# Loading routed tokens as 32-channel squares and turning them on VectorE instead of TensorE

## The chip, the cores and the metric

The kernel runs on one core of one Trainium2 chip. The metric is device time in microseconds (us) of one execution. Engines are named as the profile names them: PE is TensorE, DVE VectorE, ACT ScalarE, POOL GpSimd, SP the SyncE queue that issues most DMAs.

## What is computed

One graph layer and one transformer block over N = 4096 nodes with C = 256 channels, in fp32:

```python
h = layernorm(x);  h = concat(lin1(h), adj @ lin2(h) / degree)
h = layernorm(h)
h = h + wo(causal_attention(rmsnorm(h)))      # 4 heads, 2 kv heads, width 64, rope
g = top2(softmax(router(rmsnorm(h))))         # 8 experts
out = h + sum_e g[e] * w2[e](silu(w1[e] x) * w3[e] x),  x = rmsnorm(h), hidden width 682
```

Every token goes through two of the eight experts. The change concerns how a token's 256 channels get from the residual stream to the first matmul of its expert, where the channels have to lie on the partitions.

## The kernel before

**Stages.** The graph part ends at about 510 us of the profiled execution, attention at about 1060, and the experts at about 1522. The order on each engine is written out by hand: every engine executes its instructions in the order in which the program emits them, and waits are placed where one needs another's result.

**Lists.** While attention finishes block by block, `inputs` writes the normalized rows (L174 is `normed`), `project` adds what the first half of the router gives (L907), `residual` adds the rows to the residual stream on POOL (L917), and POOL scatters each token by indirect DMA (L1060) into `lists` in DRAM, ordered by expert. One row of `lists` has ROW = 265 words: 256 channels, the token's number, and 8 gates.

**Groups.** The experts work on 42 groups in a fixed order `TURNS`: 25 of 256 tokens and 17 of 128. All tokens of a group belong to one expert, whose weights are read at an index that the core finds in a table (`make_table`). For turn k the SP queue issues `load13` (L1382, 1.4 MB), `load2` (L1388, 0.77 MB) and `load_rows` (L1399, one DMA: 128 tokens on the partitions, one or two tokens of 265 words each). Rooms for rows and weights rotate by five; in turn k the weights of k+5 and k+4 and the rows of k+4 are loaded. `begin_experts` issues the first ones.

**One turn.** The main loop calls, for turn k, `hidden(k)` or `hidden_seven(k)`, then `combine(k-1)`, then the loads, then `sums13`, which prepares a later group's weights on POOL.

- `prepare(k+1)` is called inside the hidden part of turn k. It turns the rows on PE, four transposes of 128x128 for 256 tokens and two for 128 (L1413, tile `tx` in PSUM), ACT scales both channel halves by the norm's weights into `xT` (L1419), and DVE picks the gate of the group's expert (`pick` L1427, `gt` L1432). At which point of turn k this happens depends on which PSUM bank is free (`early`, `free_bank`).
- `hidden(k)` multiplies `xT` with w1 and w3 (L1698), ACT applies silu (L1704), DVE multiplies (L1705; L1717 for the last 42 channels).
- `hidden_seven(k)` does the same for 13 of the 256-token groups (`SPLIT13`) with seven half-size products instead of eight (L1525). It needs sums of weights, made ahead by `sums13` on POOL (L1463 to L1466), and sums of tokens T1 to T4, made by `sums_x` within `prepare` on DVE (L1480), T1 from `xT` and the PSUM tile and the others from each other and the PSUM tile. Its products are copied and added by ACT (L1531) and DVE (L1563, L1564), and L1595 and its neighbours multiply with silu.
- `split` (L1612 to L1615), `sums2` (L1631 to L1634) and `seven_products` (PE L1655, DVE L1661 to L1667) do the second layer in the same manner for all groups of 256 in `SEVEN`.
- `combine(k)` scales by the gate into `y` (ACT L1765 or DVE L1771) and POOL adds the rows into `acc_dram` by a scattering indirect DMA (L1776), after a small memset (L1775) that paces it. A small DMA from `sent` (L1911) holds SP back until then.

The copy from `acc_dram` to `out` (L1923) is issued three turns before the end; the last groups scatter into `out` itself.

In most of the stage a 256-token group of `hidden_seven` is followed by one 128-token group, whose `prepare` readies the next 256 tokens; three times two 128-token groups follow one another.

Other names that are used below: L790 is attention's exponential on ACT, L792 its mask on POOL, L810 the running sums of the softmax on DVE, L824 the products with the values on PE, L311 the transposes of the rope tables on DVE (the only DVE transposes before), `acc<-a` L532 the product with adj.

Of the kernel before, what the change touches and what calls it, by code (L numbers as in the profile page):

```python
# [10 lines left out]
I32 = mybir.dt.int32  # L11
# [55 lines left out]
def fast_kernel(  # L67
# [618 lines left out]
    with (  # L686
# [14 lines left out]
        pt_all = sp.tile([P, 9 * 1024], F32, name="pt_all")  # L701
        late = sp.tile([P, 2 * (NF + 1) * GR + 4 * GR + 5 * 2 * ROW], F32, name="late")
        LATE_XT, LATE_ROWS = 2 * (NF + 1) * GR, 2 * (NF + 1) * GR + 4 * GR
        ring = [pt_all[:, n * 1024 : (n + 1) * 1024] for n in range(9)]
# [182 lines left out]


        def inputs(b):

            row = ax.tile([P, TB, ROW], F32, tag="row", name=f"row_{b}")
            for t in range(TB):
                normed(row[:, t, 0:C], b, t, rstd[b][:, t])
            flats[b] = row

        def project(b, tiles, rooms):
            if tiles[0] == 0:
                picks[b] = small("r_p", b)
            for t, ps in zip(tiles, rooms):
                for c in range(2):  # L900
                    nc.tensor.matmul(
                        ps[:, 0 : C + NE], ys[b, c][:, t * P : (t + 1) * P], wo_sb[:, c, :],
                        start=(c == 0), stop=(c == 1),
                    )
            for t, ps in zip(tiles, rooms):
                x2 = flats[b][:, t, 0:C]
                nc.vector.tensor_add(x2, x2, ps[:, 0:C])  # L907
                nc.vector.tensor_add(picks[b][:, t, :], ps[:, C : C + NE], first_lg[b][:, t, :])
# [7 lines left out]
        def residual(b):  # L916
            nc.gpsimd.tensor_add(res[b], res[b], flats[b][:, :, 0:C])  # L917
            put = nc.sync.dma_start(acc_blocks[b], res[b])
            lend(b, "res", 4)
            if b == ORDER[-1]:  # L920
                free(put, "first sums", "the tokens of the first groups are others")
                join(put, "last x")
# [449 lines left out]
        w2s = [a.rearrange("p (k c) -> p k c", k=NF + 1) for a in at2]  # L1372
        rows, hidden_of, inputs_of, expert_of, gates_of = {}, {}, {}, {}, {}

# [11 lines left out]
        def load2(k):  # L1386
# [4 lines left out]
            )  # L1391

        def load_rows(k):
            i = TURNS[k]
            n = halves(i)
            at = entry(table[0:1, 0, i : i + 1], NE * REG - (GR if i < NW else 0))
            r = late[:, LATE_ROWS + k % 5 * 2 * ROW : LATE_ROWS + (k % 5 + 1) * 2 * ROW]
            r = r.rearrange("p (h c) -> p h c", h=HALF)
            get = nc.sync.dma_start(  # L1399
                r[:, 0:n, :], lists[bass.ds(at, n * P), :].rearrange("(h p) c -> p h c", p=P)  # L1400
            )
            if i < NA:
                free(get, "late writes", "the rows of the first groups are whole by then")
                join(get, "first reads")
            rows[i] = r

        def prepare(k, pool=p_y, tag="y"):
            i = TURNS[k]
            n = halves(i)
            tr = pool.tile([P, 2, n, P], F32, tag=tag, name=f"tx_{i}")  # L1410
            for h in range(n):
                for c in range(2):
                    nc.tensor.transpose(  # L1413
                        tr[:, c, h, :], rows[i][:, h, c * P : (c + 1) * P], ident
                    )
            xT = late[:, LATE_XT + k % 2 * 2 * GR : LATE_XT + k % 2 * 2 * GR + 2 * n * P]
            xT = xT.rearrange("p (c i) -> p c i", c=2)
            for c in range(2):
                nc.scalar.activation(  # L1419
                    xT[:, c, :], tr[:, c].rearrange("p h i -> p (h i)"), AF.Copy,  # L1420
                    scale=ln2_sb[:, c : c + 1],
                )
            inputs_of[i] = xT
            if k in SPLIT13:
                sums_x(k, tr)
            pick = ex.tile([P, n, NE], F32, tag="pick", name=f"pick_{i}")
            nc.vector.tensor_mul(  # L1427
                pick, rows[i][:, 0:n, C + 1 : ROW],
                mine[:, i : i + 1, :].to_broadcast([P, n, NE]),
# [38 lines left out]

        def sums_x(k, tr):

            xT = inputs_of[TURNS[k]]
            room = kT[6 + SPLIT13.index(k) % 2].rearrange("p (n i) -> p n i", n=4)
            m = {f"T{n + 1}": room[:, n] for n in range(4)}
            for c in range(2):
                for h in range(2):
                    m[f"B{c + 1}{h + 1}"] = xT[:, c, h * P : (h + 1) * P]
            for dst, c, h, less in (
                ("T1", 0, 1, "B11"), ("T2", 1, 1, "T1"), ("T3", 1, 1, "B12"), ("T4", 1, 0, "T2"),
            ):
                nc.vector.scalar_tensor_tensor(  # L1480
                    m[dst], tr[:, c, h, :], ln2_sb[:, c : c + 1], m[less],
                    op0=ALU.mult, op1=ALU.subtract,
# [3 lines left out]
        def hidden_seven(k, step, behind):  # L1486
# [99 lines left out]
            if behind is not None:  # L1586
                prepare(behind, p_ms, "ms")
            gated(two)
# [83 lines left out]
        def hidden(k, step=None, behind=None):  # L1672
# [3 lines left out]
            hT = hTs[k % 2][:, :, 0:n]  # L1676
            free_bank = k >= SEVEN[0]
            early = n == P and not (k - 1 in SEVEN and k - 2 in SEVEN)

            for q in range(0, NF + 1, 2):  # L1680
# [27 lines left out]
                if q == 0 and behind is not None:  # L1708
                    if not free_bank:
                        prepare(behind)  # L1710
                    elif early:
                        prepare(behind, p_ms, "ms")
                if step and q < NF - 1:
# [5 lines left out]
            )  # L1719
            if behind is not None and free_bank and not early:  # L1720
                prepare(behind, p_ms, "ms")
            hidden_of[i] = hT
# [3 lines left out]
        def combine(k):  # L1726
# [34 lines left out]
            for h in range(n):  # L1761
# [8 lines left out]
                else:  # L1770
                    nc.vector.tensor_scalar(  # L1771
                        y[:, h, :], ps[h if last else 0][:, h, :], gt[:, h], None, op0=ALU.mult
                    )
                at = bass.IndirectOffsetOnAxis(ap=r[:, h, C : C + 1].bitcast(I32), axis=0)
                nc.gpsimd.memset(gap, 0.0)  # L1775
# [13 lines left out]
        def begin_experts():  # L1789
            make_table(NB - 1, True, 0, NA)  # L1790
            load_rows(0)
            load13(0)
            load_rows(1)
            load2(0)
            load13(1)
            load_rows(2)
            load2(1)
            load_rows(3)

# [38 lines left out]
        for b in ORDER[:-1]:  # L1840
# [9 lines left out]
        later.setdefault(PLACES - 2, []).append(  # L1850
            lambda: [prepare(0, p_ms, "ms")] + [nc.gpsimd.memset(t[:, NF, :], 0.0) for t in hTs]
        )
# [36 lines left out]
        for k in range(NM):  # L1889
# [24 lines left out]
            if k + 5 < NM:  # L1914
                load13(k + 5)
            if k + 4 < NM:
                load_rows(k + 4)
            if 0 < k < NM - 1:
# [13 lines left out]
def rare_groups(  # L1932
# [34 lines left out]
    for i in range(RARE):  # L1967
# [6 lines left out]
        w2_sb = sb.tile([P, NF + 1, C], F32, tag="w2", name=f"y_w2_{i}")  # L1974
        nc.sync.dma_start(w2_sb, w2[bass.ds(e, 1)].rearrange("o p k c -> p (o k) c"))
        tr = p_y.tile([P, 2, P], F32, tag="y", name=f"y_tr_{i}")
        xT = sb.tile([P, 2, P], F32, tag="xT", name=f"y_xT_{i}")
        for c in range(2):
            nc.tensor.transpose(tr[:, c, :], r[:, c * P : (c + 1) * P], ident)
            nc.scalar.activation(  # L1980
# [684 lines left out]
```

## Time and profile before

| | |
|---|---|
| median of 3 runs | 1532.09 us (1532.08 to 1533.21) |
| the profiled execution | 1532.31 us, of which 1530.5 span |
| PE busy | 1518.1 us, 99% |
| DVE, ACT, POOL busy | 1056.4, 555.6, 556.8 us |
| DMA moved | 212.16 MB in 69595 packets |
| loads of rows, L1399 | 42 on SP |
| transposes of tokens, L1413 | 134 on PE |

The page's rows for groups of instructions read: line, engine, operation, written tile, read tiles, shape, count, then busy microseconds and the mean nanoseconds of one, then the idle time of that engine just before them and what ended it. Rows of a single line give minimum, median and maximum in nanoseconds. Rows of a timeline read: start, duration, engine, line, operation, tiles, count, and in brackets the idle time before and its releaser. Rows of a stretch read: the stretch, its length, then the busy time of PE, PE's weight loads, DVE, ACT and POOL with instruction counts, the granted clock, the DMA engines' busy share, and GB/s.

### The profile page before, as it was taken

To read this page: it belongs to the slowest core of one execution; us is meant where nothing else is said; L and a number is where in the kernel's file an instruction comes from. 1 tells how busy PE (TensorE), PEld (TensorE's weight loads), DVE (VectorE), ACT (ScalarE), POOL (GpSimd) and SP (SyncE) were. 2 spreads that over 40 slices of the span, in tenths; PEclk is the share of its full clock that TensorE was granted. 3 is DMA by queue.
4 is the path that set the end of the run, shared out by engine and by line. 5 is a ranking of instruction groups with operands and counts; after the bars stand their busy time and mean duration, and the time that the engine had idled before them with its cause. 6 is when DMAs were issued, how large, how long until landed. Compare 5 with 4: busy or idle time off the path is not lost. (4 is left out here: it accounts for less than half of the span.)

```text
span 1530.5 us, 28132 instructions
## 1 busy us (share of the span) xinstructions
PE 1518.1 (99%) x10925; PEld 1122.9 (73%) x10925; DVE 1056.4 (69%) x2182; ACT 555.6 (36%) x989; POOL 556.8 (36%) x641
## 2 busy tenths in 40 slices
PE   9999999999999999999999999999999999999997
PEld 8888888888888544444444444358899999999996
DVE  7764665755755677779879878785565777677762
ACT  2102012021021455655665655653122433343341
POOL 2102022121221331374554553442424445545342
PEclk9999999999999999999999999999999999999999
DMA  6334444543544000010011011048777787787845
GB/s 240 131 130 151 160 141 148 161 153 127 179 141 151 5 1 23 22 58 30 30 58 37 28 38 36 23 166 297 220 204 219 225 275 254 225 274 248 271 129 134
DMA packets 69595, 212.16 MB, mean 139 GB/s; under 512 B 17898, under 2 KB 45930, under 8 KB 55818
## 3 DMA queue, kind: packets, MB, share of 16 engines
q1 hardware_dynamic: 55914, 191.99, 36.4%
q0 software_dynamic: 12720, 17.47, 6.5%
q8 instruction: 88, 1.44, 0.4%
q10 hardware_dynamic: 816, 0.79, 0.2%
q14 instruction: 57, 0.47, 0.1%
HBM read 184.48 MB, written 27.13 MB: 138 GB/s over the span
## 5 line engine op out<-in xcount | busy, mean ns | idle before, releaser
L782 PE MATMUL sc<-qT_all,kT 64*64 64x512 f32 (+3 forms) x2304 | 282.1, 557 | 0.5 <-ACT pt_all L790 0.3
L532 PE MATMUL acc<-a,g 128*128 128x256 f32 x1024 | 244.0, 379 | 0.0
L532 PEld LDWEIGHTS acc<-a,g 128*128 128x128 f32 x1024 | 193.5, 190 | 31.8 <-issue 6.7
L782 PEld LDWEIGHTS sc<-qT_all,kT 64*64 64x64 f32 x2304 | 91.2, 133 | 128.6 <-issue 109.2
L790 ACT ACTIVATE pt_all<-sc 128x1024 f32<-128x1024 f32 (+3 forms) x157 | 148.8, 955 | 96.7 <-PE sc L782 94.6
L1776 POOL DMA_INDIRECT acc_dram<-y,late x40 | 62.8, 1571 | 178.0 <-ACT y L1765 118.5
L532 PE MATMUL acc<-more_sums,g 128*128 128x256 f32 x512 | 126.3, 379 | 0.0
L810 DVE TENSOR_TENSOR late<-late,pt_all 128x1024 f32<-128x1024 f32 (+3 forms) x91 | 107.5, 1181 | 24.3 <-POOL pt_all L792 9.8
L433 ACT COPY qT_all<-tr 128x512 f32<-128x512 f32 x30 | 16.2, 588 | 259.1 <-PE tr L431 259.1
L532 PEld LDWEIGHTS acc<-more_sums,g 128*128 128x128 f32 x512 | 97.2, 190 | 13.2
L824 PE MATMUL y_first<-pt_all,vv 64*64 64x512 f32 (+3 forms) x448 | 106.6, 554 | 0.0
L625 POOL TENSOR_TENSOR rot<-rot,tables 128x512 f32<-128x512 f32 x21 | 33.9, 1615 | 198.6 <-ACT rot L621 158.4
L1698 PE MATMUL h<-late,qT_all 128*128 128x256 f32 (+1 forms) x616 | 105.2, 327 | 0.0
L824 PE MATMUL y_second<-pt_all,vv 64*64 64x512 f32 (+3 forms) x436 | 104.2, 555 | 0.0
L1698 PEld LDWEIGHTS h<-late,qT_all 128*128 128x128 f32 x616 | 94.0, 191 | 9.6 <-ACT late L1419 0.8
L1060 POOL DMA_INDIRECT lists<-row,slots x64 | 87.4, 1366 | 17.1 <-issue 14.3
L1705 DVE TENSOR_TENSOR late<-si,h 128x256 f32<-128x256 f32 (+2 forms) x87 | 40.0, 467 | 73.7 <-ACT si L1704 42.7
L1704 ACT ACTIVATE si<-h 128x256 f32<-128x256 f32 (+2 forms) x87 | 36.5, 421 | 145.1 <-PE h L1698 142.2
L824 PE MATMUL y_third<-pt_all,vv 64*64 64x512 f32 (+3 forms) x372 | 88.7, 555 | 0.0
L621 ACT ACTIVATE rot<-pq 32x512 f32<-32x512 f32 x84 | 49.5, 589 | 82.6 <-DVE qT_all L619 43.6
L810 DVE TENSOR_TENSOR sum_all<-sum_all,pt_all 128x1024 f32<-128x1024 f32 (+3 forms) x51 | 56.0, 1097 | 15.5 <-POOL pt_all L792 9.2
L790 ACT ACTIVATE late<-sc 128x1024 f32<-128x1024 f32 (+3 forms) x55 | 50.9, 927 | 41.4 <-PE sc L782 38.4
(490 smaller groups left out, 3350.7 us busy)
## 6 DMA issues: line engine op xcount, KB each, us to landing
a<-in_adj_dram SPq DMA_DIRECT2D x64, 1024.0 KB
qT_all<-in_w_dram SPq DMA_DIRECT2D x18, 1408.0 KB
pt_all<-in_w_dram SPq DMA_DIRECT2D x16, 1408.0 KB
res_all<-in_w_dram SPq DMA_DIRECT2D x17, 768.0 KB
pt_all<-in_w_dram SPq DMA_DIRECT2D x16, 768.0 KB
res_all<-in_w_dram SPq DMA_DIRECT2D x8, 1408.0 KB
qT_all<-in_w_dram SPq DMA_DIRECT2D x9, 768.0 KB
late<-lists SPq DMA_DIRECT2D x25, 265.0 KB
```

What stands on the lines that cost most here:

```text
L532: nc.tensor.matmul(acc[bank][:, at, :], g[jb][:, right, k, :], m[left][:, k, :], start=(jb == 0 and k == 0 and at == 0), stop=(jb == NB - ...
L621: nc.scalar.activation(rot[n * Q : (n + 1) * Q, :], pj[(n ^ 1) * Q : ((n ^ 1) + 1) * Q, :], AF.Copy, scale=1.0 if n % 2 else -1.0,)
L625: nc.gpsimd.tensor_mul(rot, rot, tables[b][:, 1, :])
L782: nc.tensor.matmul(ps[k * HP : (k + 1) * HP, j, :w], kT[sb][hd, i * P + k * HP : i * P + (k + 1) * HP], qT[b][hd, p, off:], start=True, st ...
L790: nc.scalar.activation(pt[:, :, :w], ps[:, :, :w], AF.Exp, scale=HD ** -0.5)
L810: nc.vector.tensor_add(sums[b, p][:, :, off:], before[:, :, off:], pt[:, :, : 512 - off])
L824: nc.tensor.matmul(accs[b, p][k][hd, off:], vv[sb][some, i, hd], pt[some, j, : 512 - off], start=(s == order_of(b)[0]), stop=(s == order_o ...
L1060: put = nc.gpsimd.indirect_dma_start(out=lists[:, :], out_offset=bass.IndirectOffsetOnAxis(ap=chosen[b][:, k, t, :], axis=0), in_=flats[b] ...
L1698: nc.tensor.matmul(ps[m % 2][:, m // 2 - q, :], w13_sb[:, c, m * P : (m + 1) * P], xT[:, c, :], start=(c == 0), stop=(c == 1),)
L1704: nc.scalar.activation(si[:, 0:both, :], ps[0][:, 0:both, :], AF.Silu)
L1705: nc.vector.tensor_mul(hT[:, q : q + both, :], si[:, 0:both, :], ps[1][:, 0:both, :])
L1776: put = nc.gpsimd.indirect_dma_start(out=(acc_dram if k < NM - LAST else out)[:, :], out_offset=at, in_=y[:, h, :], in_offset=None, comput ...
```

## The change

The rows of `lists` hold the 256 channels in another order: eight pieces of 32 channels are laid out so that word (g, c, d) of a row is channel c*128 + g*32 + d, with g from 0 to 3 and c 0 or 1. `inputs` writes rows in this order, `project` adds in it, and `residual` becomes two POOL additions, one for each c, which bring the order back.

A group is then loaded by five DMAs instead of one. `load_squares` issues four, one for each g: 32 partitions, partition i holding, for every m, the 64 consecutive words (c, d) of token 32*m + i, that is pieces of 256 bytes. `load_rows` loads the remaining 9 words of each token (pieces of 36 bytes). In this layout every 32x32 square that DVE turns leaves channels g*32 + d on the partitions, so `prepare` is one DVE transpose of 128x512 (or 128x256) from SBUF to SBUF. ACT and `sums_x` read its result `turned` from SBUF where they read `tx` from PSUM before. `turned` lies in the room of the squares four turns on. No PSUM bank is needed, so `prepare` in `hidden` always comes after the first of the three steps of its loop (q == 0). `begin_experts` issues load13(0) first, then squares 0 and 1, load2(0), load13(1), rows 0 and 1, squares 2, load2(1), squares 3, rows 2 and 3.

```diff
 def residual(b):
-    nc.gpsimd.tensor_add(res[b], res[b], flats[b][:, :, 0:C])
+    x2 = flats[b][:, :, 0:C].rearrange("p t (g c d) -> p c t g d", g=4, c=2)
+    for c in range(2):
+        sums = res[b][:, :, c * P : (c + 1) * P].rearrange("p t (g d) -> p t g d", d=Q)
+        nc.gpsimd.tensor_add(sums, sums, x2[:, c])
...
+def squares_room(k):
+    return late[:, LATE_Z + k % 5 * 2 * C : LATE_Z + (k % 5 + 1) * 2 * C]
...
+def load_squares(k):
+    i = TURNS[k]
+    n = halves(i)
+    at = rows_at[i] = entry(
+        table[0:1, 0, i : i + 1], NE * REG - (GR if i < NW else 0)
+    )
+    z = squares_room(k)[:, 0 : n * C].rearrange("p (m e) -> p m e", e=2 * Q)
+    tokens = lists[bass.ds(at, n * P), 0:C].rearrange("(m i) (g e) -> g i m e", i=Q, g=4)
+    for g in range(4):
+        loaded(i, nc.sync.dma_start(z[g * Q : (g + 1) * Q], tokens[g]))
...
-def prepare(k, pool=p_y, tag="y"):
+def prepare(k):
     i = TURNS[k]
     n = halves(i)
-    tr = pool.tile([P, 2, n, P], F32, tag=tag, name=f"tx_{i}")
-    for h in range(n):
-        for c in range(2):
-            nc.tensor.transpose(
-                tr[:, c, h, :], rows[i][:, h, c * P : (c + 1) * P], ident
-            )
+    turned = squares_room(k + 4)[:, 0 : n * C]
+    nc.vector.transpose(turned, squares_room(k)[:, 0 : n * C])
+    turned = turned.rearrange("p (m c i) -> p c m i", c=2, i=Q)
...
     for c in range(2):
         nc.scalar.activation(
-            xT[:, c, :], tr[:, c].rearrange("p h i -> p (h i)"), AF.Copy,
-            scale=ln2_sb[:, c : c + 1],
+            xT[:, c, :].rearrange("p (m i) -> p m i", i=Q), turned[:, c], AF.Copy, scale=ln2_sb[:, c : c + 1]
         )
...
     if k in SPLIT13:
-        sums_x(k, tr)
+        sums_x(k, turned)
...
             nc.vector.scalar_tensor_tensor(
-                m[dst], tr[:, c, h, :], ln2_sb[:, c : c + 1], m[less],
+                four(m[dst]), turned[:, c, 4 * h : 4 * h + 4], ln2_sb[:, c : c + 1],
+                four(m[less]),
                 op0=ALU.mult, op1=ALU.subtract,
             )
...
         if q == 0 and behind is not None:
-            if not free_bank:
-                prepare(behind)
-            elif early:
-                prepare(behind, p_ms, "ms")
+            prepare(behind)
...
 def begin_experts():
     make_table(NB - 1, True, 0, NA)
-    load_rows(0)
     load13(0)
-    load_rows(1)
+    load_squares(0)
+    load_squares(1)
     load2(0)
     load13(1)
-    load_rows(2)
+    for k in range(2):
+        load_rows(k)
+    load_squares(2)
     load2(1)
-    load_rows(3)
+    load_squares(3)
+    for k in range(2, 4):
+        load_rows(k)
...
     if k + 4 < NM:
+        load_squares(k + 4)
         load_rows(k + 4)
```

Four sites more follow the new order of channels and hold no further operations: the three reads of the token's number and gates, and a path for rare groups, which isn't taken with these inputs.

## The prediction

> **What bounds the kernel now.** I read the page's busy times first, then stretches of 40 us of the expert stage, then the groups that the change touches.
>
> ```profile
> PE 1518.1 (99%) x10925; PEld 1122.9 (73%) x10925; DVE 1056.4 (69%) x2182; ACT 555.6 (36%) x989; POOL 556.8 (36%) x641
> ...
> 1200.00:1240.00 40.00, 40.00 (x331) 39.17 (x331) 27.63 (x67) 15.81 (x40) 20.57 (x22) 1.00 0.82 256
> ...
> L1413 PE MATMUL tx<-ident,late 128*128 128x128 f32 x134 | 21.6, 273 | 0.0
> ...
> L1427 DVE TENSOR_TENSOR pick<-late,mine x42: 159/165/2231, 1029.7 to 1498.3; 128x16 f32<-128x16 f32 x25, 128x8 f32<-128x8 f32 x17
> ...
> L311 DVE STREAM_TRANSPOSE tables<-tables x14: 659/680/704, 111.1 to 470.0; 32x512 f32<-32x512 f32 x14
> ```
>
> PE never rests (40.00 of 40 us), DVE works 27.6 and the DMA engines 0.82. So whatever PE sheds is a gain, if no other engine makes PE wait. An average share can't tell that; two places in the timeline can. The first is the start of the experts:
>
> ```profile
> 1026.40 0.84 ACT L1419 ACTIVATE late<-tx,ln_sb 128x256 f32<-128x256 f32 x2 [2.28 <-PE tx L1413]
> 1027.53 3.72 PE L1698 MATMUL h<-late,qT_all 128*128 128x256 f32 x16
> 1027.99 1.75 DVE L810 TENSOR_TENSOR sum_all<-sum_all,pt_all 128x256 f32<-128x256 f32 x2
> 1029.66 0.17 DVE L1427 TENSOR_TENSOR pick<-late,mine 128x16 f32<-128x16 f32 x1
> ```
>
> The first group's tokens go PE, ACT, PE and hidden(0) starts at 1027.53. DVE is behind by then: it works off softmax sums (L810) without a pause until 1029.74, and the pick of prepare(0), its next instruction, runs only then. The second place is a pair of a 256-token group in seven products and the 128-token group after it:
>
> ```profile
> 1462.28 0.16 DVE L1427 TENSOR_TENSOR pick<-late,mine 128x8 f32<-128x8 f32 x1
> 1462.42 1.55 POOL L1465 TENSOR_TENSOR sum_all<-pt_all,sum_all 128x640 f32<-128x640 f32 x1
> 1462.55 1.97 DVE L1563 TENSOR_TENSOR late<-qT_all,hy 128x512 f32<-128x512 f32 x1
> ...
> 1467.34 0.60 PE L1413 MATMUL tx<-ident,late 128*128 128x128 f32 x4
> 1467.78 3.29 PE L1698 MATMUL h<-late,pt_all 128*128 128x128 f32 x28
> ...
> 1475.79 0.29 DVE L1666 TENSOR_TENSOR vv<-vv,ye_ms 128x128 f32<-128x128 f32 x1 [0.56 <-PE ye_ms L1655]
> 1476.44 1.03 ACT L1765 ACTIVATE y<-vv,gt 128x256 f32<-128x256 f32 x2 [2.39 <-DVE vv L1667]
> 1477.37 0.56 ACT L1531 COPY wqkv_sb<-hA 128x512 f32<-128x512 f32 x1
> 1478.27 0.94 PE L1525 MATMUL hA<-kT,sum_all 128*128 128x128 f32 x7
> ...
> 1368.40 1.55 POOL L1465 TENSOR_TENSOR sum_all<-qT_all,sum_all 128x640 f32<-128x640 f32 x1
> 1368.46 1.51 DVE L1427 TENSOR_TENSOR pick<-late,mine 128x8 f32<-128x8 f32 x1
> ```
>
> Four transposes hold PE 0.44 us (1467.34 to 1467.78), so 0.11 each, not the 273 ns of the group. From 1462 to 1477 DVE rests once, 0.56 us before L1666; ACT's y waits for DVE, the copy L1531 follows y on ACT, and PE's second product needs that copy: it ends at 1477.94, a hand-over takes 0.15, and PE, by its own pace due at 1478.27, gets there 0.18 us later. A DVE chain longer by more than 0.55+0.18 = **0.73 us** stops PE here.
>
> [...] a 165 ns pick took 1.51 us when it came 0.06 us after POOL's L1465, and L1563 took 1.97 behind it, 0.68 elsewhere. [...] In a window with one 1 MB adj load and two table loads, packets took 66.6% of 6 us x 16 = 63.9 us; 128 adj packets at 374 ns are 47.8, so 128-byte ones cost about 15.7 ns.[...]
>
> **The parts.** The sum is against the profiled execution, 1532.31 (span 1530.5 and 1.8 around it), 0.2 above the median 1532.09.
>
> - PE loses 134 transposes, 0.11 us each. The last 4 lie behind the copy of acc_dram to out, whose scatters end the kernel on POOL: nothing. The others gain where nothing makes PE wait.
> - The transpose's own price: the 680 ns row has 32 partitions, the new one 128. The pitch of two in a row is 0.65, which I take[...]. Below 0.65 nothing speaks for.[...]
> - Start: begin_experts puts load13(0) ahead of the rows, and eight square loads among the weights on SP. The DVE order of the changed kernel puts the transpose behind all L810, thus at 1029.74. Plus 0.65 (680 ns less overlap), ACT's two scalings 0.84, 0.05 hand-over: PE starts at 1031.28 instead of 1027.53, **+3.75**, the first four transposes' gain included. The squares have until 1029.74; SP issues them from about 1018 at 0.38 each, with 1.4 MB of weights, which before landed within 8.2 us.
> - prepare(1): -0.44. The 36 transposes of the groups until 1182: **-3.96**; DVE has over a third of that stretch free.
> - Pairs. In a single 128-group the order is L1705, transpose, four sums (L1480), pick. The transpose adds 0.65, and T1 needs the scaled copy, so DVE also waits ACT's 0.84 and two hand-overs, about 0.95: +1.6 to the chain. In the seven products the 256-column transpose (estimate 0.35, half of the row) pushes the pick, which came 0.14 before POOL's L1465, about 0.2 behind it: blocked, as at 1368.46; that pair's L1595 ended 0.93 later than its peers. So 1.6+0.93-0.73 = +1.8 for each of **6** pairs (after 1202, 1274, 1296, 1368, 1441, 1462), **+10.9**, with the 6x0.11 not gained. The pair at 1187 has the +1.6 alone: **+0.9**.
> - Three single groups (1257, 1351, 1424) have no L1465 near and over 2 us of rest on DVE: -2.0. Three cases with two 128-groups after one another (1223, 1317, 1390; 8 transposes): -2.6. The group at 1483: -0.4.
> - T3 and T4 now have two SBUF inputs instead of one and PSUM, so POOL's L1463 can block them: 0 to +0.8 for each of the three doubles. [...] I take +0.5 for both.
> - DMA: 1024 pieces of 256 bytes per 256-group. Between 15.7 ns (128 bytes) and 64 ns (the 1060-byte rows) I take 22: 1.4 us of 16 engines, less 1.0 for the rows' packets, plus 0.2 for the 36-byte ones: +0.6 of some 12.5 us, share 0.82 to 0.87. Hidden. Four more issues on SP are 1.5 us per group (0.38 each), and the next group's load2 and load13 come after them; but SP waits up to 11.8 us at a time for the gap memset, so they are hidden. The transpose waits for four DMAs where PE waited for one: with a late square, DVE's activations' products, sums2 and the adds behind it would all stand, then PE; loads are issued three groups, some 35 us, ahead.
> - Attention: residual becomes two POOL adds (2.2 to 2.9 us together before, +0 to +1), inputs and project only change order within rows; none is waited for by PE. Zero; without that cover +8.
>
> Sum: 3.75-0.44-3.96+10.9+0.9-2.0-2.6-0.4+0.5 = **+6.6**: 1538.9 profiled, 1538.7 median.
>
> **The rivals.**
>
> 1. Locks are worse: T3/T4 and more two-input operations meet POOL; the doubles lose their 0.88 and 0.8 more, and each pair another hand of 0.2: about +6, 1545. L1563's 1.97 speaks for it; its neighbours with a PSUM input were never slowed.
> 2. The pick still slips in ahead of POOL (L1465 waits for the same moment in the seven products): pairs pay 1.6-0.73 = 0.9, 5.6 less in all: +1.0, 1533.1.
> 3. Faster: the DVE chain of the pairs stays within 0.73 us, in one place, prepare in the 128-group. If ACT's scaling from SBUF and T1 overlap more than I think, PE never waits there, and all seven pairs gain 0.66: 10.9+0.9+4.6 = 16.4 less, 9.8 under before, 1522. It decides at 0.73 of added chain; the transposes alone are 0.65+0.35, so it needs reads from SBUF to give back 0.3 and hide the wait for ACT. Against it: T1 now begins 0.04 after ACT.
> 4. Small packets: at 64 ns a piece, as the rows, 1024 cost 4.1 us, +3.1 per 12.5 us and a share over 1: DMA binds, about +18, 1557. It decides from 55 ns; the 15.7 speaks against it.
>
> That the turn isn't done by DVE at all is excluded: its order in the changed kernel has 42 transposes, one per group.
>
> **How the numbers follow.** The forecast 0.43, its own range 1534 to 1546; locks 0.15; pick ahead 0.20; no wait in the pairs 0.18; packets 0.04. Something like 0.2% (3.1 us) is what a measurement of this kernel can tell. Slower: 0.40+0.15+0.04+0.04 = 0.63; within: 0.03+0.13+0.01 = 0.17; faster: 0.03+0.17 = 0.20. The range leaves out the packets and most of rival 3: 1524 to 1547.
>
> **What would show it.** Right: hidden(0) starts near 1031, led by DVE; the second seven-products copy waits for ACT's y, PE rests 1 to 2 us in six pairs; picks of 1 to 1.5 us are many. Wrong: PE busy through 1200 to 1480 (rival 3), PE waiting for squares by DMA (rival 4), or the L1413 gain missing in 1060 to 1160.

## The result, and the profile after

The changed kernel takes 1545.08 us (median of 5 runs, 1540.64 to 1547.17) against 1532.53 for the kernel before (1532.08 to 1533.21): a ratio of 1.0076, 95% interval 1.0056 to 1.0097. It is slower by 12.5 us, and its runs lie 6.5 us apart where those of before lie 1.1 apart. The profiled execution took 1541.60 (span 1539.8), 9.3 more than the one of before. The prediction was slower, by 6.6.

Line numbers differ from those of before: the weight sums L1463 to L1466 on POOL are now L1491 to L1494, the pick L1427 is L1455, ACT's scaling L1419 is L1448, the sums of tokens L1480 are L1512, the seven products L1525 are L1558 with their copies L1564, L1563 is L1596, L1698 is L1728. In the experiments below they move by some lines more; the tiles' names stay.

The changed kernel's page, busy time by engine:

```profile
PE 1509.4 (98%) x10791; PEld 1113.9 (72%) x10791; DVE 1085.2 (70%) x2224; ACT 554.4 (36%) x989; POOL 556.6 (36%) x649
```

One stretch of its expert stage:

```profile
1200.00:1240.00 40.00, 37.93 (x307) 36.98 (x308) 29.84 (x66) 15.03 (x39) 21.55 (x24) 1.00 0.83 230
```

And the rows of two lines (minimum, median and maximum in ns):

```profile
L1443 DVE STREAM_TRANSPOSE late<-late x42: 435/703/707, 1030.7 to 1501.5; 128x512 f32<-128x512 f32 x25, 128x256 f32<-128x256 f32 x17
...
L1455 DVE TENSOR_TENSOR pick<-late,mine x42: 123/166/2000, 1037.8 to 1502.1; 128x16 f32<-128x16 f32 x25, 128x8 f32<-128x8 f32 x17
```

PE runs 134 instructions fewer and is busy 8.7 us less, in a longer span: it now rests, 2.1 us in this stretch of 40. The transpose costs DVE 0.70 us for 512 columns and 0.44 for 256; the row of before with 32 partitions and 512 columns has 0.68. The timeline shows three kinds of place where PE rests. The first is the start of the experts:

```profile
1030.72 0.70 DVE L1443 STREAM_TRANSPOSE late<-late 128x512 f32<-128x512 f32 x1
1031.46 0.91 ACT L1448 ACTIVATE late<-late,ln_sb 128x256 f32<-128x256 f32 x2 [6.73 <-DVE late L1443]
1032.02 6.42 PE L1728 MATMUL h<-late,qT_all 128*128 128x256 f32 x16 [4.56 <-ACT late L1448]
...
1037.82 0.18 DVE L1455 TENSOR_TENSOR pick<-late,mine 128x16 f32<-128x16 f32 x1 [6.39 <-DMA late<-lists]
```

The same place in stretches of 4 us; the third figure from the end is the granted clock:

```profile
1028.00:1032.00 4.00, 0.00 (x0) 0.00 (x0) 3.22 (x4) 0.54 (x2) 0.00 (x0) 0.84 0.97 330
1032.00:1036.00 4.00, 3.98 (x9) 3.16 (x10) 0.00 (x0) 2.12 (x3) 0.00 (x0) 0.50 1.13 267
```

DVE's transpose comes behind the softmax sums, and PE rests 4.56 us, as forecast. Not forecast: the granted clock then is 0.50, and the first 16 products take 6.42 us instead of 3.72. The second place is a pair of a 256-token and a 128-token group, here the last of seven:

```profile
1470.99 0.44 DVE L1443 STREAM_TRANSPOSE late<-late 128x256 f32<-128x256 f32 x1
1471.28 1.54 POOL L1493 TENSOR_TENSOR sum_all<-pt_all,sum_all 128x640 f32<-128x640 f32 x1
1471.35 1.50 DVE L1455 TENSOR_TENSOR pick<-late,mine 128x8 f32<-128x8 f32 x1
1472.96 1.91 DVE L1596 TENSOR_TENSOR late<-qT_all,hy 128x512 f32<-128x512 f32 x1
...
1479.26 0.70 DVE L1443 STREAM_TRANSPOSE late<-late 128x512 f32<-128x512 f32 x1
1480.54 0.35 DVE L1512 SCALAR_TENSOR_TENSOR kT<-late,ln_sb 128x128 f32<-128x128 f32 x1 [0.58 <-ACT late L1448]
...
1486.89 1.03 ACT L1790 ACTIVATE y<-vv,gt 128x256 f32<-128x256 f32 x2 [4.79 <-DVE vv L1700]
...
1487.83 0.56 ACT L1564 COPY wqkv_sb<-hA 128x512 f32<-128x512 f32 x1
...
1488.49 1.13 PE L1558 MATMUL hA<-kT,sum_all 128*128 128x128 f32 x8 [2.01 <-issue]
```

The transpose pushes the pick 0.07 us behind POOL's L1493, and it takes 1.50 us instead of 0.16: it ends at 1472.85, 0.03 after L1493. A DVE operation that takes longer in this way while one of POOL's weight sums runs is called held below (locked out, in the expectations). L1596 behind it takes 1.91, much as its counterpart L1563 did before (1.97), but it starts later. In the 128-group the transpose and a wait of 0.58 for ACT come ahead of T1. What follows on DVE is late: ACT's y waits 4.79 us for it (2.39 before), the copy L1564 comes behind y, and PE rests 2.01 us ahead of the second product. The profile names no releaser for that rest ("issue"); that it is the copy follows from the copy's end at 1488.39, 0.10 us before PE goes on (the working took 0.15 for this hand-over). Six pairs have a rest of 1.82 to 2.13 us, the pair at 1187 one of 0.83. The third place is the pair after two 128-groups, at two of its three occurrences:

```profile
1246.18 0.35 DVE L1512 SCALAR_TENSOR_TENSOR kT<-late,ln_sb,kT 128x128 f32<-128x128 f32 x1
1246.50 1.62 POOL L1491 TENSOR_TENSOR res_all<-pt_all 128x640 f32<-128x640 f32 x1
...
1412.93 3.01 DVE L1512 SCALAR_TENSOR_TENSOR kT<-late,ln_sb 128x128 f32<-128x128 f32 x1 [0.58 <-ACT late L1448]
1413.66 2.12 POOL L1491 TENSOR_TENSOR sum_all<-qT_all 128x640 f32<-128x640 f32 x1
...
1426.07 1.38 PE L1558 MATMUL hA<-kT,pt_all 128*128 128x128 f32 x10 [1.24 <-DVE hy L1567]
```

At 1246 the last T sum is issued 0.32 us before L1491, and all four take 0.35. At 1412.93 T1 takes 3.01 and the other three 1.6 to 1.7, POOL's four sums in between, and PE rests 1.24 us in the next group, waiting for `hy`, which DVE adds up. (T1 begins 0.73 us before L1491 here; what held it that early the trace doesn't show.) In the third occurrence, at 1341, two of the T sums take 2.35 and 1.68 us and PE doesn't rest.

### The profile page after: what moved, and what is told of

Same layout as the page of the kernel before. It is cut to its first block, busy times and chain, and to the rows that moved or that the text cites. A ratio compares the mean times of both kernels' runs of the same rounds, so it can differ in the third digit from the quotient of the medians.

```text
span 1539.8 us, 28601 instructions
## 1 busy us (share of the span) xinstructions
PE 1509.4 (98%) x10791; PEld 1113.9 (72%) x10791; DVE 1085.2 (70%) x2224; ACT 554.4 (36%) x989; POOL 556.6 (36%) x649
## 4 chain that ended last, share of the span: by engine, by line
PE 93%; DMA 2%; DVE 2%; issue 1%; POOL 1%; ACT 0%; SPq 0%; DVEq 0%; POOLq 0%; ACTq 0%
PE acc L532 25%; PE sc L785 14%; PE h L1728 13%; PE y_second L827 5%; PE y_third L827 4%; PE y_first L827 4%; PE ye_y L1779 4%; PE hA L1558 4%; PE ye_y L1688 3%; PE ye_ms L1688 2%; PE pq L612 2%; PE pf L503 2%; PE hD L1558 2%; PE ph L193 2%; PE po L913 1%
## 5 line engine op out<-in xcount | busy, mean ns | idle before, releaser
L1728 PE MATMUL h<-late,qT_all 128*128 128x256 f32 (+1 forms) x616 | 106.7, 333 | 4.6 <-ACT late L1448 4.6
L1728 PEld LDWEIGHTS h<-late,qT_all 128*128 128x128 f32 x616 | 95.4, 194 | 15.0 <-ACT late L1448 5.4
```

The costliest lines, as they stand in the source:

```text
L1728: nc.tensor.matmul(ps[m % 2][:, m // 2 - q, :], w13_sb[:, c, m * P : (m + 1) * P], xT[:, c, :], start=(c == 0), stop=(c == 1),)
```

## The experiments

Medians and ratios are against runs of the kernel before that were taken beside them on the same chip; its medians there were 1532.54 to 1532.80, so that times of different experiments can be compared to some 0.3 us. Most kernels share this split of `prepare`, which by itself leaves the order as it is:

```diff
+def turn(k):
+    n = halves(TURNS[k])
+    turned_of[k] = squares_room(k + 4)[:, 0 : n * C]
+    nc.vector.transpose(turned_of[k], squares_room(k)[:, 0 : n * C])
 def prepare(k):
+    if k not in turned_of:
+        turn(k)
```

**e1_start: the start alone.**

```diff
+            load_squares(0)
             load13(0)
-            load_squares(0)
             load_squares(1)
...
+        later.setdefault(PLACES - 6, []).append(lambda: turn(0))
```

> Only the start of the experts is mended: squares(0) are loaded ahead of load13(0), and DVE turns them six places earlier, ahead of the last softmax sums; the rest is as changed. Theory (PE waits for DVE at the start, and the wait also costs clock): the 4.56 us of rest ahead of the first L1728 goes, and so does the half clock of the first 16 products (6.42 instead of 3.72 us, 2.7 us), together 7 us: about 1536 instead of 1545, and the scatter between runs shrinks. Rival (the clock falls there for another reason, such as the load on DMA): only 4.5 us come back, 1540, and the products at half clock stay.

Measured: 1545.26 (1543.35 to 1547.99), ratio 1.0082 (1.0067 to 1.0097). Neither the theory's 1536 nor the rival's 1540. The timeline of e1_start:

```profile
1028.82 3.69 PE L1735 MATMUL h<-late,qT_all 128*128 128x256 f32 x16 [1.90 <-DMA qT_all<-in_w_dram]
...
1036.38 0.17 DVE L1462 TENSOR_TENSOR pick<-late,mine 128x16 f32<-128x16 f32 x1 [5.61 <-DMA late<-lists]
...
1044.16 1.25 PE L913 MATMUL po<-wo_sb,yT 128*128 128x264 f32 x2 [3.40 <-DVE yT L849]
```

And its stretch behind the last wait:

```profile
1044.00:1048.00 4.00, 3.84 (x11) 3.09 (x12) 3.25 (x10) 0.76 (x2) 0.00 (x0) 0.58 1.01 425
```

The wait for DVE is gone, and two others take its place. The weights, now behind the squares, come 1.90 us late; and DVE stands 5.61 us at the first pick for the 9-word rows, which `begin_experts` issues behind squares, weights and more squares. Everything behind the pick on DVE is late, among it the reciprocal, and PE waits 3.40 us for it; then the granted clock is 0.58 in the stretch. After the wait of 1.90 the 16 products took 3.69 us, so that wait cost no clock. In the changed kernel the pick had waited too, but PE was so late itself that it didn't show. All in all this order gained next to nothing at the start: PE's second product of the first pair begins at 1199.80 where it began at 1200.08.

**e2_pick: the pick ahead of the transpose in the seven products.**

```diff
+            if k - 1 in SPLIT13:
+                gate(k)          # pick and gt
             if k not in turned_of:
                 turn(k)
```

> In the seven products only, pick and gt stand ahead of the transpose instead of behind it; all else as changed. Theory (the transpose pushes the pick behind POOL's L1493, and it is locked out): pick is 0.16 us again, L1628 ends 1.1 us sooner after the second product, and six waits of PE of 1.8 to 2.1 us become about 0.8: 6 to 7 us less, about 1538. Rival (the adds L1596 are locked out anyway, so the pick's place is no matter): PE's waits stay at 1.8 to 2.1, 1545.

Measured: 1537.00 (1534.87 to 1539.21), 1.0029 (1.0017 to 1.0041). The six waits of PE are 0.90 to 1.06 us instead of 1.82 to 2.13, for instance

```profile
1222.13 1.13 PE L1573 MATMUL hA<-kT,res_all 128*128 128x128 f32 x8 [1.06 <-issue]
```

(the second product after 1202). So half of each wait was the held pick; this is 6 x 0.95 = 5.7 of the 8 us. The rest is not separated; shorter waits can also spare PE stretches at half clock, which followed nine of 34 rests of 1.82 to 2.15 us and none of these (e11_double).

**e3_turn: the transpose ahead of split, or at the head of the 128-group.**

```diff
             hidden_of[i] = hT
+            if k + 2 in SPLIT13 and TURNS[k + 1] >= NW:
+                turn(k + 2)
             split(k, hT)
...
+            if behind in SPLIT13 and n == P and behind not in turned_of:
+                turn(behind)
             for q in range(0, NF + 1, 2):
```

> The 256-column-halves of a group that follows a 128-group are turned one step sooner: the transpose of 512 columns stands ahead of split, or at the head of hidden, so that ACT's scaling is done when DVE comes to T1; the pick stays behind the transpose in the seven products. Theory (0.58 us of DVE's delay per pair is the wait for ACT, and the locked T sums come from being late): six waits become about 1.3, the wait of 1.24 in the pair after a double goes: about 4.5 us less, 1540. Rival (DVE's amount of work alone decides): no change, 1545.

Measured: 1534.59 (20 runs, 1533.60 to 1536.15), 1.0012 (1.0005 to 1.0019): 10.5 less, more than forecast. The six waits are 0.85 to 0.86, the one of 1.24 doesn't occur, and new ones of 0.18 to 0.37 appear for L1657 (split's sums, which now stand behind the transpose). DVE runs the same 2224 instructions as in the changed kernel; the rival falls.

**e4_all: these together, with the turn in the seven products where DVE rests.**

```diff
+            if behind is not None:
+                turn(behind)
             begun(two)
             third(one)
```

(and e1_start, e3_turn)

> All three together: start mended, the turn ahead of split or hidden in the 128-groups, and in the seven products the turn moved ahead of the second half's first products, where DVE rests, so that the pick stands where it stood before the change. Theory (order, not amount of work): only 0.65 us is added to DVE's chain in a pair with 0.73 to spare, PE never waits, and the transposes taken off PE are a gain of 14 us: 1518. Rival (amount of DVE work or DMA pieces): a part of the waits stays, 1524 to 1532.

Measured: 1529.62 (1527.64 to 1532.58), 0.9983 (0.9974 to 0.9992): faster than before, but not 1518. It lies in the rival's range, though not for the rival's reasons alone: most of what stays is at the start. The waits in the pairs are 0.21 to 0.38; at the start PE waits 3.22 for weights and 2.83 behind the pick, as in e1_start.

**e5_gates and e6_filler: what the rest at the start does to the clock.**

```diff
+            if k in (1, 2):
+                gate(k - 1)
+            if k > 1:
+                gate(k)
```

and in e6_filler also

```diff
+        idle = p_ms.tile([P, TB, P], F32, tag="ms", name="idle_e")
+        for n in range(36):
+            nc.tensor.transpose(idle[:, n % TB], ident, ident)
         for k in range(NM):
```

> As changed, but pick and gt of the first two groups run one group later, so that DVE does not stand at pick(0) for the 9-word rows, which came at 1037.8 after a wait of 6.39 us. Theory (half a clock hides that wait in the changed kernel; it only shows where PE is quicker, as in the runs with the start mended, 3.4 us there): no change or up to 2 us less, 1543 to 1545, with the 6.4 us stretch of the first 16 products still there. Rival (that wait is what made the runs of the changed kernel differ by 6.5 us): 1541 and runs closer together.

> As e5_gates, with 36 transposes of the identity on PE (0.11 us each, 4 us, result unused) between the last attention product and the first product of the experts, in the time in which PE would rest. Theory (PE's rest of over 4 us is what halves the granted clock): the first 16 products take 3.7 instead of 6.4 us, 2.7 us less than e5_gates, though the rest itself is only filled. Rival (clock falls for another reason): same time as e5_gates, 6.4 us again.

Measured: e5_gates 1543.53 (1542.83 to 1548.02), e6_filler 1543.41 (1542.27 to 1546.72). In time they can't be told apart, since their runs scatter by 5 us. The timelines of the start can be, e5_gates first, then e6_filler:

```profile
1031.55 5.41 PE L1743 MATMUL h<-late,qT_all 128*128 128x256 f32 x16 [4.56 <-ACT late L1466]
```

```profile
1026.96 4.15 PE L1933 MATMUL idle_e<-ident 128*128 128x128 f32 x36
1031.14 3.72 PE L1743 MATMUL h<-late,qT_all 128*128 128x256 f32 x16
```

With PE kept busy, the same 16 products begin 0.4 us sooner and take 3.72 us instead of 5.41, and the granted clock in 1032 to 1036 is 1.00 instead of 0.57; so it is PE's rest that lowers the clock here. Over the kernels with this rest of 4.56 to 4.59 us the 16 took 5.41 (e5_gates), 5.80 (e11_double), 6.23 (e3_turn), 6.42 (the changed kernel) and 6.58 (e2_pick): 1.7 to 2.9 us lost, varying.

**e10_warm: the same in time**, on e3_turn, whose runs lie closer together (its edit with those of e5_gates and e6_filler).

> e3_turn (1534.6, the turn sooner in 128-groups) with pick and gt of the first two groups one group later and the 36 filling transposes of e6_filler. Theory (half a clock after PE's rest at the start cost 1.7 to 2.7 us; without the locked T sums the runs differ little, so that it shows in the time): 1532 to 1533. Rival (the filled rest gives nothing in time, something behind it takes it back): 1534 to 1535.

Measured: 1532.12 (12 runs, 1531.49 to 1532.74), 0.9996 (0.9988 to 1.0005): 2.5 less than e3_turn, with runs 1.3 us apart instead of 2.6. In e3_turn's timeline the 16 products take 6.23 - 3.72 = 2.51 us longer, the same amount, so that the moved gates, which e10_warm has as well, need not explain any of it. The half clock at the start is worth some 2.5 us, and part of the scatter.

**e7_pieces and e9_pieces: the small pieces alone, in the kernel before.**

```diff
+            for c0, c1 in ((0, 64), (64, 128), (128, 192), (192, 256), (256, ROW)):
+                get = nc.sync.dma_start(r[:, 0:n, c0:c1],
+                    lists[bass.ds(at, n * P), c0:c1].rearrange("(h p) c -> p h c", p=P))
```

> The kernel before with one part of the change alone: each load of rows is split into four of 64 channels and one of 9 words per token, so that a group of 256 tokens makes 1024 pieces of 256 bytes and 256 of 36, and five issues on SP instead of one; PE still turns. Theory (small pieces are hidden, save at the start where DMA is the bound): within 0 to 3 us of before, 1532.7 to 1536, and no wait of PE from 1200 to 1480. Rival (pieces carry a good part of the loss): 1537 or more.

Measured: 1586.11, 1.0354 (1.0328 to 1.0381), far beyond both. SP's queue and PE in e7_pieces:

```profile
1203.54 13.81 SPq L1400 DMA_DIRECT2D late<-lists  x5
...
1219.42 0.87 PE L1415 MATMUL tx<-ident,late 128*128 128x128 f32 x3 [4.25 <-DMA late<-lists]
```

Five issues of 0.38 us take 13.81, so that (13.81 - 5 x 0.38)/4 = 2.98 us lie between two of them; a transfer of `lists` took 2.6 us at least to land, 3.6 in the median. For 256 tokens the column ranges interleave in the room. That each is taken as overlapping the one before, so that its issue waits for that one to land, is a reading of these numbers; no row shows it. The experiment measured those waits, not the pieces. In e9_pieces the places don't interleave:

```diff
+                for h in range(n):
+                    for c0, c1 in ((0, 64), (64, 128), (128, 192), (192, 256), (256, ROW)):
+                        get = nc.sync.dma_start(r[:, h, c0:c1], tokens[:, h, c0:c1])
```

> The kernel before with the small pieces alone, without the waits that e7_pieces had between them: from the fifth group on, rows are loaded one half at a time in pieces of 64 channels and of 9 words, ten issues for 256 tokens, whose places on the chip do not interleave; the first four groups are loaded as before. Theory (256-byte pieces are hidden behind 35 us of lead and a DMA share under 1): within 2 us of before, no wait of PE for rows. Rival (pieces bind the DMA engines or the SP queue): 5 us slower or more, with PE's transposes waiting for late<-lists.

Measured: 1532.93 (12 runs), 1.0000 (0.9992 to 1.0009), with 103920 packets instead of 69595, and in the stretch

```profile
1200.00:1240.00 40.00, 40.00 (x331) 39.17 (x331) 27.64 (x67) 15.71 (x40) 20.58 (x22) 1.00 0.84 249
```

PE is busy 40 of 40 us. The pieces of all but the first four groups cost nothing.

**e11_double and e12_both: the scatter.** e11_double has only this of e3_turn; e12_both adds e5_gates and the filler.

```diff
+            if behind in SPLIT13 and n == P and k - 1 not in SPLIT13:
+                turn(behind)
```

> As changed, but in the second 128-group of the three doubles alone the turn stands at the head of hidden, ahead of the first product, so that the T sums come before POOL's L1491. Theory (a T sum locked out by POOL costs 1.24 us of PE's time and the 0.66 that are not gained, in none to three of the doubles from run to run): no wait for hy ahead of the last products, runs within 2 us of each other, at or below the fastest of the changed kernel, 1539 to 1541. Rival (the scatter has another source, such as the clock): runs still 5 us apart, median 1543 or more.

Measured: 1539.28 (1537.61 to 1542.81), 1.0046 (1.0029 to 1.0063). No wait for hy is left and the median is below the fastest run of the changed kernel, but the runs are still 5.2 apart: the theory's cost holds, its claim on the scatter only in part. In e11_double's timeline the T sums pass ahead of POOL (L1519 and L1498 here are L1512 and L1491):

```profile
1412.89 0.34 DVE L1519 SCALAR_TENSOR_TENSOR kT<-late,ln_sb,kT 128x128 f32<-128x128 f32 x1
...
1413.93 2.12 POOL L1498 TENSOR_TENSOR sum_all<-qT_all 128x640 f32<-128x640 f32 x1
```

One more source of scatter stands in the traces: the rests in the pairs can cost clock as well. In this execution PE rests 1.84 us before 1293.91 and 2.15 before 1463.71, and goes on with the same sequence of products:

```profile
1293.91:1297.91 4.00, 4.00 (x24) 4.00 (x25) 1.31 (x2) 1.51 (x4) 3.81 (x5) 0.67 0.53 54
1295.25:1298.66 3.41, 3.41 (x19) 3.41 (x18) 0.69 (x1) 0.94 (x3) 3.33 (x4) 0.50 0.74 89
1463.71:1467.71 4.00, 4.00 (x35) 4.00 (x36) 1.69 (x3) 1.62 (x5) 3.81 (x5) 1.00 0.55 57
```

In the 4 us behind the rest PE runs 24 products in the one case and 35 in the other. The half clock lasts 3.41 us, and the 30 products behind the rest take 5.05 us instead of 3.42. Of the 34 rests of 1.82 to 2.15 us in the pairs of six traces, nine were followed by it: none of six in the changed kernel's profiled execution, two in e1_start, one in e5_gates, three in e6_filler, two in e11_double, one in e12_both. It did not follow the rests of up to 1.25 us in e2_pick and e3_turn. For six such rests this is, as an estimate, 6 x 9/34 x 1.63 = 2.6 us in the mean of many executions.

> As changed, with e11_double's earlier turn in the three doubles, pick and gt of the first two groups one group later, and e6_filler's 36 transposes: the two things that the runs of e11_double and e6_filler pointed to as sources of the scatter are both gone, the six locked picks are not. Theory (locked T sums in the doubles and the length of the half clock at the start are the scatter, the six picks the rest of the loss): 1536 to 1538, runs within 2.5 us, six waits of PE of 1.8 to 2.1 us still there. Rival (a third source of scatter, for instance whether a pick is locked out at all): runs still 4 to 5 us apart.

Measured: 1538.38 (1536.90 to 1539.68), 1.0040 (1.0026 to 1.0053). The runs are 2.8 apart instead of 6.5, the six waits of 1.85 to 2.14 remain, one of them with the half clock behind it. So T sums and the clock at the start are the greater part of the scatter. What is left fits the half clock behind the six waits; no run separates it.

**e8_best: what the runs pointed to.** e4_all, and

```diff
-            load13(0)
-            load_squares(0)
-            load_squares(1)
-            load2(0)
-            load13(1)
-            for k in range(2):
-                load_rows(k)
+            load_squares(0)
+            load13(0)
+            load_rows(0)
+            load13(1)
+            load_squares(1)
+            load_rows(1)
+            load2(0)
...
             sums2(k)
+            gate(k)
             begun(one)
```

with the gates of the first two groups as in e5_gates.

> e4_all with the start ordered anew (squares 0, load13(0), rows 0, load13(1), squares 1, rows 1, load2(0), then the others), pick and gt of the first two groups one group later, and pick and gt of the groups in seven products at the head of hidden_seven, where DVE rests. Theory (what is left of the waits in e4_all is 3.2 us for weights and 2.8 us behind pick(0) at the start, with 1.3 us of half clock, and 0.2 to 0.4 in each pair): PE waits at most 2 us at the start, and the time falls to about 1520. Rival (DMA cannot bring squares and weights by then, in whatever order): 3 us and more of waits stay at the start, 1525 or more.

Measured: 1522.49 (1521.08 to 1523.53), 0.9936 (0.9923 to 0.9950): 10.3 us faster than the kernel before, with the same transposes on DVE and the same pieces. The stretch in e8_best:

```profile
1200.00:1240.00 40.00, 39.94 (x324) 38.85 (x323) 30.77 (x74) 14.02 (x37) 21.38 (x24) 1.00 0.86 248
```

And its timeline at the start of the experts:

```profile
1028.04 3.69 PE L1750 MATMUL h<-late,qT_all 128*128 128x256 f32 x16 [1.14 <-DMA qT_all<-in_w_dram]
```

In this stretch DVE is busier than in the changed kernel (30.77 against 29.84), and PE waits 0.06 us. At the start PE waits 1.14 us for weights and later 0.37 for DVE, and behind that there is no rest of 0.15 us or more; the granted clock is 1.00 in every stretch of 40 us from 1000 to 1480. Loads, gates and turns were all moved here at once; what each gives alone is known only from the experiments above.

## Why the prediction was right or wrong

The mechanism was right: DVE's longer chain stops PE at the start and in six pairs, and this outweighs the transposes that PE sheds. Of the signs that were named, hidden(0) started at 1032.02 behind DVE, six rests were 1.82 to 2.13 us, and ten of 42 picks took 1.3 to 2.0. That the sum came within 2.7 us of the profiled execution is in part luck: the start was put 2.8 too low and the groups around the doubles 2.3, the six pairs 1.9 too high. The median, 1545.08, is 6.4 above the forecast, near the upper end of the range, and is rival 1's number without being its account, since the pairs came out cheaper.

The terms are measured as the difference of PE's start times at the same instruction in the two profiled timelines: dn (L839, now L842), hA<-late of the first pair, and each later hA<-kT.

| term | predicted | measured |
|---|---|---|
| before the experts | 0 | +0.6 |
| start, with prepare(1) | +3.3 | +6.1 |
| the groups until 1182 | -4.0 | -4.3 |
| the pair at 1187 | +0.9 | +1.0 |
| six pairs | +10.9 | +9.0 |
| three doubles | -2.6 | -2.5 |
| three single groups after them | -2.0 | +0.2 |
| 1483 and the end | -0.4 | -0.9 |
| allowance (an estimate) | +0.5 | in the rows above |
| sum | +6.6 | +9.3 |

- **Before the experts.** PE's warm-up transposes L642 took 5.83 us instead of 4.83, and 0.62 of it is still there at 15 us; the program is the same there. It is no part of the change.
- **Start: the mechanism was right, the term too small.** dn moved from 1031.61 to 1038.37, 6.1 without the 0.6. PE starts at 1032.02, 1031.4 without the 0.6, where 1031.28 was worked out; what the prediction left out is the clock behind it, 6.42 - 3.72 = 2.70. In the traces a rest of 3.22 us (e4_all), of 3.40 (e1_start) and of 4.56 (the changed kernel) was followed by a granted clock of 0.66, 0.58 and 0.50 in the stretch of 4 us at or behind the point where PE goes on (1032 to 1036, 1044 to 1048, 1032 to 1036). Rests of 1.90 in e1_start and 2.83 in e4_all were followed by 1.00, but nine of 34 rests of 1.82 to 2.15 us by half clock, as shown under e11_double, so that in these runs the length of a rest alone doesn't tell. The working priced a rest of over 4 us at its own length; the profile before has no such rest in the experts' stage from which the clock's part could have been read.
- **Six pairs: right in place, number and cause, each a little dear.** The six waits stand where the prediction put them. Each pair is longer by 1.24 to 1.70 us, not 1.8. In the pair from 1465.38 to 1488.49 the end of the multiplications moved from 9.98 to 11.13 us after the second product, 1.15 where 0.93 was taken; but T1 waits for one of ACT's two scalings only, 0.58 us where 0.95 was taken. (Six times 1.8 is 10.8, not 10.9.) e2_pick shows the first part (0.95 of each wait), e3_turn the second. Which of the two operations started first doesn't settle it: a pick 0.07 us behind L1493 took 1.50, and four T sums of which the last began 0.32 us ahead of L1491 took 0.35 each; but T1 at 1412.93 took 3.01 though it began 0.73 ahead.
- **Doubles: the term for T sums was wrong in its place.** In the profile before, L1564, with one input in PSUM, took 0.69 us in all 13 executions of 128x512, eight of them while POOL's L1466 ran, where L1563, with both in SBUF, took up to 2.03; the T sums, with one input in PSUM, took 0.34 to 0.35 in all 52. With both in SBUF they took 0.34 to 3.01 in the changed kernel. The 0 to 0.8 was put in the doubles, where it did not show (-2.5); it shows one group later, where PE waits 1.24 for hy and the 0.66 isn't gained, near 2 us each. One of three was so in the profiled execution, two in e5_gates, three in e1_start and e6_filler. This is rival 1 in a milder form. That the median is 3.5 above the profiled execution can come from these T sums and from the half clock behind the rests in the pairs, of which that execution had none; the shares of the two are not shown.
- **DMA.** The cost of the pieces held: e9_pieces is level with before, and the share of 1200 to 1240 is 0.83 where 0.87 was the forecast. The packets' times in the traces are 13.0 ns for 128 bytes and 49.5 for 1060 (means, before), less than the 15.7 and 64 of the working, and 22.9 for 256 bytes (changed kernel, 1100 to 1500), where 22 was taken. "Hidden" did not hold at the start, where the prediction only asked whether the squares came by 1029.74. They did; the 9-word rows did not come until 1037.8, a transfer that the working did not follow. In 1024 to 1028 the DMA engines move 193 GB/s at a share of 1.01 where before it was 413 at 1.03.
- **Rivals.** The pick that slips in ahead is excluded by the held picks; DMA as the bound of the groups by e9_pieces. The faster case, in which the pairs' chain keeps within 0.73 us, did not happen in this order, and reads from SBUF gave nothing back (ACT's scaling 0.49 us in the median of all groups, 0.47 from PSUM before; a T sum that isn't held 0.35, 0.34 before); e8_best reaches it by another order, not by slack that was there.

## What to carry to other kernels

Taking work off the busiest engine is worth its pace there only if the engine that gets it has room at that point of its own order; the same transposes lost 12.5 us where they stood and gained 10.3 when they were issued where DVE rested and the first loads and gates were put in another order. When an edit lets a short operation slip by a few tenths of a microsecond, look for an operation of another engine that it can now run into, as a pick of 0.16 us took 1.50 beside POOL here, and for a rest of the matrix engine that costs clock as well as time; here nine of 34 rests of 1.82 to 2.15 us did. When loads are split, follow the smallest piece too: here it went last, and its reader on DVE stood 5.61 us in e1_start, with all that came behind it.

## What the runs showed of the hardware that was not expected

- A rest of PE of 4.56 to 4.59 us cost 1.7 to 2.9 us more in the 16 products behind it; 36 transposes with unused results in that rest took this away.
- A rest of 1.82 to 2.15 us was followed in nine of 34 cases by a stretch at half clock; the one shown has 0.50 for 3.41 us and cost 1.63. Within one execution it followed some of these rests and not others.
- Some DMA issues on SP are long: the squares' L1426 takes 0.34 us in the median and 1.55 at most, the 9-word rows' L1433 0.39 and 5.59. The longest stands at 1054.86, where the DMA engines' share is 1.02 (1052 to 1056); but weights issued at 1043.68 to 1046.53, at a share of 1.00 and 1.01 (1040 to 1044 and 1044 to 1048), took 0.33 each, so that a full share alone doesn't do it.
- Two DVE operations in a row can be held: in the pair shown the pick took 1.50 while L1493 ran, and L1596 right behind it 1.91 (0.68 at the least) while L1494 ran, which had begun at 1472.78. Before the change the pick took 0.16 there, and only L1563 was held (1.97), while L1465 ran.
